# A GNN layer on one core: gathers in four parts a group with a bound lead, and 47 instead of 21 tiles fetched by row

## The chip, the core and the metric

The kernel runs on one core of one Trainium2 chip. The core has five engines with an instruction stream each: TensorE (PE in the profile; PEld is its weight load), VectorE (DVE), ScalarE (ACT), GpSimd (POOL) and SyncE (SP). They meet through semaphores. Any of SP, ACT and POOL can issue DMA transfers; the data is moved by 16 DMA engines. The metric is the device time of one execution, in microseconds (us); less is better.

## The reference

One pre-norm layer of a graph network over N = 12500 nodes of D = 256 features and E = 200000 edges, all in fp32. `dst` is sorted.

```python
h = jnp.maximum(_layernorm(x, axis=-1), 0.0)
agg = jax.ops.segment_sum(h[src], dst, num_segments=N)
z = (1.0 + eps_gin) * h + agg
t = jnp.dot(z, W1) + b1                          # 256 -> 512
t = jax.nn.relu(_batchnorm(t, g1, bt1))
conv_out = jnp.dot(t, W2) + b2                   # 512 -> 256
out = x + jax.nn.relu(_batchnorm(conv_out + h, g2, bt2))
```

The part that matters here is `h[src]` with its sum: for each of 200000 edges a row of 1 KB is fetched from a node's place and added to the edge's target.

## The kernel before

**Tiles and groups.** The edges are cut into 1563 tiles of 128 (NTILE) and the tiles into 131 groups (NG) of 12 (GT). As `dst` is sorted, a tile's edges go to few neighbouring nodes. A tile of gathered rows is 128 x 256: an edge on each partition.

**Three stretches.** The first 30 groups (LEAD) gather from `x` and normalize what they gathered, while another part of the program computes h for all nodes and writes it to a table, `h_one`. Groups 30 to 130 gather finished rows from `h_one`; this is the middle stage, from 518.4 to 2282.0 us in the profiled execution. Behind it come the batch norm, the second product and the output.

**One step of the loop (lines 826 to 879).** Step i issues the gathers of group i+4 (AHEAD = 4) on POOL (`gather`, L573), builds the one-hot matrices of group i+2 on DVE (`edges`, L635), and sums group i on PE (`sums`, L655). `sums` does one matmul for each tile, `ps += oh^T x rows`, with the one-hot matrix as weights: 12 weight loads and 12 matmuls (L672) add up in one PSUM tile `ps`. Then DVE copies `ps` to `zs` (`hold`, L726), PE places `zs` in the columns of its nodes (`put`, L733, L739) and DVE adds that to `zc` (`add`, L754), which holds h itself, loaded on SP (`z_load`, L629) and scaled on ACT (`z_scale`, L633). When a chunk of `zc` is complete PE multiplies it with W1 (`slice_of`, L764), DVE takes its moments (L775) and ACT stores it (`keep_t`, L782). `put` and `slice_of` stand among the matmuls of `sums`.

**Gathers.** A tile is one indirect DMA on POOL (L589): it reads 128 row numbers of `srcT` and writes 128 rows. A group's twelve go to one buffer of `rows_pool`, which has four (RING = 4), so POOL may be up to four groups ahead of PE. POOL does little else in the middle stage. The gathers' arrival is kept by hand: all but the last of a group count on a semaphore `inside` that nobody waits for, the last one on a semaphore of its buffer, `landing[place_of(i)]` (L516 to L521), and TensorE waits for that once ahead of a group's first matmul (`wait_for`, called at L660). `behind` tells the scheduler that this wait covers the group's tiles.

**Tiles by row.** Some tiles are fetched another way, one row at a time, by SP or ACT (`fetch`, L553). `SINGLES` (L32) says which: SP has a tile in group 33 and each ninth group from there (11 tiles), ACT in group 37 and each ninth (10): 21 tiles that POOL doesn't gather, always the group's first ones, summed last. A tile is made in four pieces of 32 rows (PIECE). A piece loads 32 byte offsets into the engine's registers (L560, a TENSOR_LOAD) and issues 32 DMAs of 1 KB (L565), each of which counts on `arrived[k]`; TensorE waits for the whole tile ahead of its matmul (L671). The pieces are due from step i-7 on (SOONER = 7), spread over the steps of one spacing (L551), behind the loads of that step. The places are the twelve tiles of two buffers that are free by then, `gta` (8) and `gtb` (4), in turn. In the profile the rows of L565 and the matmuls `ps<-gta,oh` and `ps<-gtb,oh` are these tiles.

**What sets the order.** Each engine runs its instructions in the order of the program. On SP the `zc` loads and the rows share one stream, on ACT the scaling of `zc`, the stores of `ts` and the rows.

Of the kernel before, what the change touches and what calls it, by code (L numbers as in the profile page):

```python
# [17 lines left out]
P = 128  # L18
# [4 lines left out]
AHEAD = 4  # L23
LEAD = 30
EARLY = 2
FRONT = 2
RING = 4
# [1 line left out]
XIN = 1  # L29
PIECE = 32  # L30
SOONER = 7
SINGLES = (("sync", 33, 9), ("scalar", 37, 9))  # L32


COPIES = 2
# [6 lines left out]
def kernel(  # L42
# [16 lines left out]
    nc = tc.nc  # L59
# [10 lines left out]
    for g in range(NCH):  # L70
        rows = min(CH, N - g * CH)
# [7 lines left out]
    full_tiles = E // P  # L79
    left = E - full_tiles * P  # L80
    NG = -(-NTILE // GT)
# [8 lines left out]
    h_one = dram.tile([N, D], F32, name="h_one")  # L90
# [25 lines left out]
    srcT = consts.tile([P, NBLK * P], I32, name="srcT")  # L116
# [49 lines left out]
    with ExitStack() as es:  # L166
# [5 lines left out]
        whole = E // PART  # L172
# [67 lines left out]
        for i in range(EARLY):  # L240
            for t in reversed(range(GT)):
                k = i * GT + t
                nc.gpsimd.indirect_dma_start(
                    out=slot(early[i], t), out_offset=None, in_=x,
                    in_offset=bass.IndirectOffsetOnAxis(ap=srcF if k == GT - 1 else srcE[:, k : k + 1], axis=0),
# [103 lines left out]
    def fast():  # L349

        parts = []
        for n0, w in chunks:
            n = w * R
# [20 lines left out]
        with ExitStack() as fs:  # L374
# [10 lines left out]
            h_one = dram.tile([N, D], F32, name="h_one")  # L385
# [4 lines left out]
            with ExitStack() as es:  # L390
# [122 lines left out]

                groups = [(t0, min(GT, NTILE - t0)) for t0 in range(0, NTILE, GT)]
                gathered = {i: early[i] for i in range(EARLY)}
                landing = [tc.alloc_semaphore(f"whole{k}") for k in range(AHEAD + 1 + RING)]  # L516
                inside = tc.alloc_semaphore("inside")
                uses, arrival = [0] * len(landing), {}

                def place_of(i):  # L520
                    return i % (AHEAD + 1) if i < LEAD else AHEAD + 1 + i % RING  # L521

                singles_at = [
                    (tile_, c) for tile_ in lands[0] for c in range(tile_.shape[1])
# [1 line left out]
                alone, due = {}, {}  # L526
                for name, i0, every in SINGLES:
                    for k in range(NG):
# [24 lines left out]
                def fetch(name, step):  # L553

                    eng = getattr(nc, name)
                    for i, j, q in due.pop((name, step), ()):
                        k, _ = placing[i, j]
                        place, c = singles_at[k]
                        k_line = i - opening
                        _, ats = nc.values_load_multi_w_load_instructions(  # L560
                            starts[j][k_line : k_line + 1, q : q + PIECE], engines=[eng.engine],
                            min_val=0, max_val=(N - 1) * ROW, skip_runtime_bounds_check_because="src names nodes",
                        )
                        for r, at in enumerate(ats):
                            single = eng.dma_start(  # L565
                                place[q + r : q + r + 1, c, :].bitcast(U8),
                                h_bytes[bass.ds(at, ROW)].rearrange("(o b) -> o b", o=1),
                            )
                            tc.no_tile_sem_insts.add(single.ins.name)
                            tc.add_to_no_dep_group(f"single{i}_{j}", single.ins)  # L570
                            single.then_inc(arrived[k], 16)

                def gather(i):  # L573
                    t0, n = groups[i]
                    a = len(alone.get(i, ()))
                    k = i % (AHEAD + 1)
                    if i >= LEAD:
                        pair = rows_pool.tile([P, 2 * GT, D], F32, name="gt")
                        ga = [(a, GT, pair[:, a:GT, :])]
                        for j in range(a):  # L580
                            place, c = singles_at[placing[i, j][0]]
                            ga.append((j, j + 1, place[:, c : c + 1, :]))
                    elif k < EARLY:
                        ga = early[k]
                    else:
                        ga = ((0, GT, singles[k - EARLY]),)
                    for t in reversed(range(t0 + a, t0 + n)):
                        rows = left if t == full_tiles else P
                        fetch = nc.gpsimd.indirect_dma_start(  # L589
                            out=slot(ga, t - t0)[:rows], out_offset=None, in_=x if i < LEAD else h_one,  # L590
                            in_offset=bass.IndirectOffsetOnAxis(ap=srcT[:rows, t : t + 1], axis=0),
                        )
                        if i < NG - 2:
                            tc.no_tile_sem_insts.add(fetch.ins.name)
                            tc.add_to_no_dep_group(f"rows{i}", fetch.ins)
                            fetch.then_inc(inside if t > t0 + a else landing[place_of(i)], 16)
                    if i < NG - 2:
                        uses[place_of(i)] += 1
                        arrival[i] = landing[place_of(i)], 16 * uses[place_of(i)]
                    gathered[i] = ga  # L600

                def wait_for(i, eng):

                    if i in arrival:
                        eng.wait_ge(*arrival.pop(i))
                        return True

                def behind(i, reader):

                    tc.declare_no_dep(reader.ins, group=f"rows{i}", reason="its engine waits for the group's semaphore")  # L610
                    tc.declare_fence(reader.ins, group=f"rows{i}")

                def span(i):
                    return STEP * i - MARGIN, STEP * i - MARGIN + WIDE
# [11 lines left out]
                def z_load(c):  # L626
                    n = chunks[c][1] * R
                    zc[c] = zcp.tile([P, DC, CH], F32, name="zc")
                    nc.sync.dma_start(zc[c][:, :, :n], h_cols[c, :, :, :n])  # L629
# [19 lines left out]
                def sum_place(i):  # L649
                    if not halves:  # L650
                        pair = ps_s.tile([P, 2, D], F32, name="ps")
                        halves.extend((pair[:, 1, :], pair[:, 0, :]))
                    return halves.pop()

                def sums(i, among=()):  # L655

                    t0, n = groups[i]
                    ga, oh = gathered.pop(i), ohs.pop(i)
                    waited = wait_for(i, nc.tensor)
                    ps = sum_place(i)  # L660
                    a = sum((i, j) in placing for j in range(n))
                    order = list(reversed(range(a + 1, n))) + list(reversed(range(a))) + [a]
                    at = {(k + 1) * n // (len(among) + 1): work for k, work in enumerate(among)}
                    for k, j in enumerate(order):
                        if k in at:
                            at[k]()
                        rows = left if t0 + j == full_tiles else P
                        lhsT, rhs = oh[:rows, j, :], slot(ga, j)[:rows]
                        if (i, j) in placing:
                            place, use = placing[i, j]  # L670
                            nc.tensor.wait_ge(arrived[place], 16 * P * use)  # L671
                        part = nc.tensor.matmul(ps, lhsT=lhsT, rhs=rhs, start=(j == order[0]), stop=(j == order[-1]))  # L672
                        if waited:
                            behind(i, part)
                            waited = False
                        if (i, j) in placing:
                            tc.declare_no_dep(part.ins, group=f"single{i}_{j}", reason="TensorE waits for their own semaphore")
                            tc.declare_fence(part.ins, group=f"single{i}_{j}")
                    summed[i] = ps
# [119 lines left out]
                def first(c):  # L799

                    return min(i for i in range(NG) if c in reach(i))
# [6 lines left out]
                for i in range(EARLY, min(AHEAD, NG)):  # L808
                    gather(i)
# [10 lines left out]
                for c in range(NCH):  # L820
                    k = min(max(first(c) - 2, c + 2), NG - CLOSE - 1)
# [4 lines left out]
                for i in range(NG - CLOSE):  # L826
# [49 lines left out]
                    for c in loads.get(i, ()):  # L876
                        z_load(c)
                    for name, _, _ in SINGLES:
                        fetch(name, i)
# [96 lines left out]
            with tc.tile_pool(name="ps_y", bufs=2, space=PSUM, reuse_waits="tile") as ps_y:  # L976
# [117 lines left out]
                for p in range(1, PAIRS - 1):  # L1094
                    a, b = 2 * p, 2 * p + 1
# [47 lines left out]
                a, b = 2 * p, 2 * p + 1  # L1143
# [308 lines left out]
    with tc.If(off == 0):  # L1452
        fast()
# [32 lines left out]
```

## Time and profile before

| | |
|---|---|
| runs | 2508.0, 2510.9 and 2526.5 us; median 2510.9 |
| profiled execution | 2513.2 us; its span in the profile 2511.4 us |
| mean granted clock of TensorE | 0.751 |

| stage (us) | length | POOL busy | PE busy | granted clock | DMA engines' busy share |
|---|---|---|---|---|---|
| 0 to 518.4: groups 0 to 29, h | 518.4 | 343 | 281 | 0.76 | 0.59 |
| 518.4 to 2282.0: groups 30 to 130 | 1763.6 | 1119 | 995 | 0.72 | 0.38 |
| 2282.0 to 2511.4: the rest | 229.4 | 74 | 211 | 0.98 | 0.77 |

How to read the views below. In a view by group or by timeline a row names the engine, the line, the operation, the output and inputs with the program's names, and how many; busy time and the mean of one stand beside it. `[4.52 <-remote]` behind a row is the idle time of that engine just before it and what ended it: "remote" is a semaphore from another engine that the trace can't name further, "issue" means that the engine waited for nothing that the profile shows, a name is the instruction or DMA that was waited for. A row whose engine ends in q (SPq, ACTq, POOLq) counts what the engine's queue did outside its busy time, DMA issues and waits; its numbers are the shortest, median and longest duration of one in ns, then the first and the last time. In the view of waits a row gives the waiting engine, its output and line, the releaser, the total idle time in us, how often, and the longest.

### The profile page before, as it was taken

The page shows a single profiled execution, that of the slowest core. Times are in us where ns is not written, and L with a number is a line of the kernel's source. Part 1 is how long each engine was busy: PE and PEld are TensorE (multiplying, and loading weights), DVE is VectorE, ACT ScalarE, POOL GpSimd, SP SyncE. Part 2 cuts the span into 40 slices and gives each one's busy share as a digit, 9 for nine tenths or more (in the row PEclk, how much of TensorE's full clock was granted, in tenths as well). Part 3 has the DMA queues.
Part 4 walks back from the last instruction along what each step waited for, and adds up shares of the span by engine and source line. Part 5 has one row for each costly group of instructions (what it writes and reads, how often), then busy time and mean ns, then how long its engine had stood idle before and what let it go on. Part 6 is the DMA issues. An engine that isn't in the chain of part 4 may idle for free.

```text
span 2511.4 us, 20472 instructions
## 1 busy us (share of the span) xinstructions
PE 1486.5 (59%) x4856; PEld 1016.6 (40%) x4856; DVE 860.0 (34%) x1344; ACT 419.0 (17%) x776; POOL 1536.4 (61%) x1588
## 2 busy tenths in 40 slices
PE   2456565656655655475654546555364565658997
PEld 1334343434443434343433425333252343435445
DVE  5445465532222212222221222222221222223897
ACT  4465465430000000000000000000000000001554
POOL 7666666656566666666665666656656566662550
PEclk9667787768777777676767767777676767779999
DMA  5565566533333333333333433333333333343988
GB/s 173 162 202 183 171 208 203 163 100 111 106 110 115 105 112 109 106 109 113 113 102 101 117 96 111 113 101 109 98 107 106 106 106 104 111 146 101 315 308 337
DMA packets 150561, 349.87 MB, mean 139 GB/s; under 512 B 33061, under 2 KB 63612, under 8 KB 150430
## 3 DMA queue, kind: packets, MB, share of 16 engines
q0 software_dynamic: 74000, 202.15, 28.6%
q1 hardware_dynamic: 58922, 118.77, 13.8%
q10 hardware_dynamic: 17508, 27.55, 3.0%
q8 instruction: 41, 0.67, 0.1%
q14 instruction: 90, 0.74, 0.1%
HBM read 284.33 MB, written 64.00 MB: 139 GB/s over the span
## 4 chain that ended last, share of the span: by engine, by line
issue 30%; PE 29%; ACTq 18%; another core or an unknown queue 8%; DVE 5%; ACT 4%; SPq 3%; DMA 1%; POOL 1%; DVEq 0%
ACTq L565 16%; PE ps L672 16%; PE ph L764 3%; PE pz L739 3%; SPq L565 3%; ACT gt L460 2%; PE one L1025 2%; ACTq L560 2%; PE pr L1025 1%; PE pq L1025 1%; PE ph L499 1%; DVE oh L640 1%; DVE stg L433 1%; ACTq L782 1%
## 5 line engine op out<-in xcount | busy, mean ns | idle before, releaser
L589 POOL DMA_INDIRECT gt<-h_one,srcT x1182 | 1119.3, 947 | 644.5 <-issue 348.6
L672 PE MATMUL ps<-gt,oh 128*128 128x256 f32 x2766 | 832.1, 437 | 475.6 <-issue 467.9
L672 PEld LDWEIGHTS ps<-gt,oh 128*128 128x128 f32 x2766 | 607.1, 221 | 697.9 <-issue 607.7
L726 DVE COPY zs<-ps 128x256 f32<-128x256 f32 x99 | 41.4, 418 | 814.8 <-remote 586.6
L640 DVE TENSOR_TENSOR oh<-col,dstT 128x1536 f32<-128x1536 f32 x129 | 225.6, 1750 | 238.4 <-remote 143.4
L633 ACT ACTIVATE zc<-zc,gin 128x1024 f32<-128x1024 f32 (+1 forms) x25 | 28.2, 1128 | 1537.4 <-issue 1259.4
L739 PE MATMUL pz<-at,zs 128*128 128x256 f32 x516 | 180.8, 457 | 166.1 <-issue 151.9
L589 POOL DMA_INDIRECT gt<-in_x_dram,srcT x216 | 204.6, 947 | 99.4 <-issue 45.5
L764 PE MATMUL ph<-zc,w1s 128*128 128x512 f32 (+1 forms) x392 | 209.7, 660 | 45.0 <-DVE gt L511 29.0
L739 PEld LDWEIGHTS pz<-at,zs 128*128 128x128 f32 x516 | 118.0, 230 | 215.5 <-issue 189.4
L775 DVE BATCH_NORM_STATS2 st<-ph 128x6 f32<-128x512 f32 x96 | 66.6, 693 | 266.1 <-remote 188.2
L672 PE MATMUL ps<-gta,oh 128*128 128x256 f32 x224 | 64.0, 420 | 139.5 <-DMA gta<-h_one 122.0
L754 DVE TENSOR_TENSOR zc<-pz,zc 128x512 f32<-128x512 f32 (+7 forms) x185 | 91.2, 517 | 119.6 <-remote 81.9
L764 PEld LDWEIGHTS ph<-zc,w1s 128*128 128x128 f32 x392 | 84.6, 218 | 115.2 <-issue 73.9
L460 ACT ACTIVATE gt<-gt,nbg,rsg 128x256 f32<-128x256 f32 x216 | 108.6, 592 | 10.6 <-issue 10.5
L672 PEld LDWEIGHTS ps<-gta,oh 128*128 128x128 f32 x224 | 46.5, 212 | 151.4 <-DMA gta<-h_one 125.8
L589 POOL DMA_INDIRECT gta<-in_x_dram,srcT x80 | 75.7, 947 | 37.1 <-issue 14.9
L499 PE MATMUL ph<-ident,gt 128*128 128x128 f32 x196 | 38.5, 317 | 93.3 <-issue 61.4
L672 PE MATMUL ps<-gtb,oh 128*128 128x256 f32 x106 | 40.5, 517 | 73.9 <-DMA gtb<-h_one 39.1
L499 PEld LDWEIGHTS ph<-ident,gt 128*128 128x128 f32 x196 | 26.5, 159 | 108.8 <-issue 69.1
L433 DVE BATCH_NORM_STATS2 stg<-gt 128x6 f32<-128x512 f32 x108 | 68.3, 688 | 3.2 <-DMA gt<-in_x_dram,srcT 2.6
L731 DVE TENSOR_SCALAR at<-col,shift 128x256 f32<-128x256 f32 x129 | 61.0, 474 | 1.1 <-issue 1.1
(188 smaller groups left out, 1152.2 us busy)
## 6 DMA issues: line engine op xcount, KB each, us to landing
t_tab<-ts ACTq DMA_DIRECT2D x96, 256.0 KB
gt<-h_one,srcT POOLq DMA_INDIRECT x1182
gta<-h_one SPq DMA_DIRECT2D x1024, 1.0 KB
gta<-h_one ACTq DMA_DIRECT2D x1024, 1.0 KB
gt<-in_x_dram SPq DMA_DIRECT2D x24, 512.0 KB
h_one<-gt SPq DMA_DIRECT2D x24, 512.0 KB
h_cols<-gt SPq DMA_DIRECT2D x24, 512.0 KB
zc<-h_cols SPq DMA_DIRECT2D x24, 512.0 KB
```

The source lines that it names most:

```text
L433: reader = nc.vector.bn_stats(st[:, c : c + 2, :].rearrange("p c s -> p (c s)"), two.rearrange("p c d -> p d c"),)
L460: nc.scalar.activation(slot(to, c), slot(v, c), AF.Relu, bias=nb[:, c : c + 1], scale=rs[:, c : c + 1])
L499: nc.tensor.transpose(ph[:, c * P : (c + 1) * P], ht[:, c, d * P : (d + 1) * P], ident)
L565: single = eng.dma_start(place[q + r : q + r + 1, c, :].bitcast(U8), h_bytes[bass.ds(at, ROW)].rearrange("(o b) -> o b", o=1),)
L589: fetch = nc.gpsimd.indirect_dma_start(out=slot(ga, t - t0)[:rows], out_offset=None, in_=x if i < LEAD else h_one, in_offset=bass.Indirect ...
L640: nc.vector.tensor_tensor(oh, col[:, :P].unsqueeze(1).to_broadcast([P, n, P]), dstT[:, t0 : t0 + n].unsqueeze(2).to_broadcast([P, n, P]), ...
L672: part = nc.tensor.matmul(ps, lhsT=lhsT, rhs=rhs, start=(j == order[0]), stop=(j == order[-1]))
L739: nc.tensor.matmul(pz[:, d, :n], lhsT=zs[:, d * P : (d + 1) * P], rhs=at[:, :n], start=True, stop=True)
L754: nc.vector.tensor_add(side, pz[:, :, a - lo : b - lo], side)
L764: nc.tensor.matmul(ph[:, :n], lhsT=w1s[:, d, f * P : (f + 1) * P], rhs=zc[c][:, d, :n], start=(d == 0), stop=(d == DC - 1),)
L775: nc.vector.bn_stats(st1[:, f, c, :], ph[:, :n])
L1025: nc.tensor.matmul(ps, lhsT=w[:, k, :], rhs=t[:, k, :], start=(k == 0), stop=(k == DC - 1))
```

## The change

Three things, all in the middle stage.

1. *Four parts.* A group of the middle stage is gathered in four parts (PARTS = 4) of up to three tiles. Each part has a landing semaphore of its own, and TensorE waits for a part ahead of that part's first matmul, no longer once a group.
2. *A bound lead.* TensorE counts on a new semaphore, `summed_up`, with each part that it has closed. From group 38 on (SETTLED) POOL waits ahead of each part until TensorE has closed the part five back (CLOSELY = 5). Before, only the four buffers of `rows_pool` bounded its lead.
3. *More tiles by row.* SP has a tile in group 33 and each fourth group from there (24 tiles), ACT in group 35 and each fourth (23): 47 tiles, not 21. A tile's four pieces are then due one a step, steps i-7 to i-4.

Unchanged are the number of buffers, the order of the tiles in a group, the first 30 groups and the two last ones.

```diff
+PARTS = 4
+CLOSELY = 5
+SETTLED = 38
-SINGLES = (("sync", 33, 9), ("scalar", 37, 9))
+SINGLES = (("sync", 33, 4), ("scalar", 35, 4))
...
-                landing = [tc.alloc_semaphore(f"whole{k}") for k in range(AHEAD + 1 + RING)]
+                landing = [tc.alloc_semaphore(f"whole{k}") for k in range(AHEAD + 1 + RING * PARTS)]
+                summed_up = tc.alloc_semaphore("summed_up")
...
-                def place_of(i):
-                    return i % (AHEAD + 1) if i < LEAD else AHEAD + 1 + i % RING
+                def place_of(i, part=0):
+                    return i % (AHEAD + 1) if i < LEAD else AHEAD + 1 + i % RING * PARTS + part
+
+                def parts_of(i, a, n):
+
+                    rows = list(reversed(range(a, n)))
+                    if not LEAD <= i < NG - 2:
+                        return [rows]
+                    size = -(-len(rows) // PARTS)
+                    return [rows[k * size : (k + 1) * size] for k in range(PARTS)]
...
-                    for t in reversed(range(t0 + a, t0 + n)):
...
+                    for part, members in enumerate(parts_of(i, a, n)):
+                        if SETTLED <= i < NG - 2:
+                            nc.gpsimd.wait_ge(summed_up, PARTS * (i - LEAD) + part - CLOSELY + 1)
+                        for j in members:
+                            t = t0 + j
...
+                                fetch.then_inc(landing[place_of(i, part)] if j == members[-1] else inside, 16)
...
-                    waited = wait_for(i, nc.tensor)
...
+                    opens, closes = {}, set()
+                    if i >= LEAD or (i, 0) in arrival:
+                        for part, members in enumerate(parts_of(i, a, n)):
+                            opens[members[0]] = part
+                            closes.add(members[-1])
...
+                        waited = j in opens and wait_for(i, nc.tensor, opens[j])
...
                         part = nc.tensor.matmul(ps, lhsT=lhsT, rhs=rhs, start=(j == order[0]), stop=(j == order[-1]))
                         if waited:
-                            behind(i, part)
-                            waited = False
+                            behind(i, part, opens[j])
+                        if i >= LEAD and j in closes:
+                            nc.tensor.sem_inc(summed_up, 1)
```

`wait_for` and `behind` take a part beside the group; nothing else of them changes.

More of the change, by code (lines that the diff above doesn't have):

```diff
@@ L586, in gather @@
                         ga = ((0, GT, singles[k - EARLY]),)
-                    for t in reversed(range(t0 + a, t0 + n)):
[L588 to L592, printed above, removed]
-                        if i < NG - 2:
-                            tc.no_tile_sem_insts.add(fetch.ins.name)
-                            tc.add_to_no_dep_group(f"rows{i}", fetch.ins)
-                            fetch.then_inc(inside if t > t0 + a else landing[place_of(i)], 16)
@@ L597, in gather @@
-                    if i < NG - 2:
-                        uses[place_of(i)] += 1
-                        arrival[i] = landing[place_of(i)], 16 * uses[place_of(i)]
+                    for part, members in enumerate(parts_of(i, a, n)):
[3 more added lines that the diff above has]
+                            t = t0 + j
+                            rows = left if t == full_tiles else P
+                            fetch = nc.gpsimd.indirect_dma_start(
+                                out=slot(ga, j)[:rows], out_offset=None, in_=x if i < LEAD else h_one,
+                                in_offset=bass.IndirectOffsetOnAxis(ap=srcT[:rows, t : t + 1], axis=0),
+                            )
+                            if i < NG - 2:
+                                tc.no_tile_sem_insts.add(fetch.ins.name)
+                                tc.add_to_no_dep_group(f"rows{i}_{part}", fetch.ins)
+                                fetch.then_inc(landing[place_of(i, part)] if j == members[-1] else inside, 16)
+                        if i < NG - 2:
+                            uses[place_of(i, part)] += 1
+                            arrival[i, part] = landing[place_of(i, part)], 16 * uses[place_of(i, part)]
@@ L600, in gather, with wait_for @@
                     gathered[i] = ga
-                def wait_for(i, eng):
-                    if i in arrival:
-                        eng.wait_ge(*arrival.pop(i))
-                        return True
-                def behind(i, reader):
-                    tc.declare_no_dep(reader.ins, group=f"rows{i}", reason="its engine waits for the group's semaphore")
-                    tc.declare_fence(reader.ins, group=f"rows{i}")
+                def wait_for(i, eng, part=0):
+                    if (i, part) in arrival:
+                        eng.wait_ge(*arrival.pop((i, part)))
+                        return True
@@ L613, in span, with behind @@
+                def behind(i, reader, part=0):
+                    tc.declare_no_dep(reader.ins, group=f"rows{i}_{part}", reason="its engine waits for their semaphore")
+                    tc.declare_fence(reader.ins, group=f"rows{i}_{part}")
                 def span(i):
```

## The prediction

> **What bounds the kernel now.** I read the times first, then the page's span and its 40 slices, then the busy time by stage.
>
> ```profile
> span 2511.4 us, 20472 instructions
> ...
> POOL 7666666656566666666665666656656566662550
> PEclk9667787768777777676767767777676767779999
> ...
> core 0: us, PE busy (x) PEld busy (x) DVE busy (x) ACT busy (x) POOL busy (x), PEclk, DMA share, GB/s
> 518.40:2282.00 1763.60, 994.73 (x3132) 691.13 (x3132) 411.70 (x612) 44.01 (x66) 1119.32 (x1182) 0.72 0.38 108
> 2282.00:2511.40 229.40, 210.63 (x702) 117.61 (x700) 184.25 (x244) 109.34 (x146) 74.09 (x34) 0.98 0.77 278
> ```
>
> The edit lies in the middle stage, 518.4 to 2282.0: 1763.6 us with all 1182 gathers from `h_one`. No engine is full in it: POOL is busy for 1119 us, PE for 995, the DMA engines for 38%. So I looked at what starts each gather: the costliest group, then the timeline of POOL, where I kept the first gather after each pause.
>
> ```profile
> L589 POOL DMA_INDIRECT gt<-h_one,srcT x1182 | 1119.3, 947 | 644.5 <-issue 348.6
> ...
> 1453.46 0.95 POOL L589 DMA_INDIRECT gt<-h_one,srcT  x1 [4.52 <-remote]
> ...
> 1487.97 0.94 POOL L589 DMA_INDIRECT gt<-h_one,srcT  x1 [4.78 <-remote]
> ...
> 1768.64 0.95 POOL L589 DMA_INDIRECT gt<-h_one,srcT  x1 [4.62 <-remote]
> 1786.16 0.95 POOL L589 DMA_INDIRECT gt<-h_one,srcT  x1 [2.81 <-remote]
> ...
> 2193.26 0.96 POOL L589 DMA_INDIRECT gt<-h_one,srcT  x1 [4.43 <-remote]
> 2244.34 0.95 POOL L589 DMA_INDIRECT gt<-h_one,srcT  x1 [6.28 <-remote]
> ```
>
> A gather takes 0.95 us and about 0.30 of issue, 1.25 together. From 1453.46 to 1487.97 that is 24 gathers and a pause of 4.78, from 1768.64 to 1786.16 it is 12 and 2.81, from 2193.26 to 2244.34 it is 36 and 6.28. The pause grows with the run: 34.51 / 24 = 1.438 us a gather, 17.52 / 12 = 1.46, and 51.08 / 36 = 1.419 in the last one, behind the last single row. So a gather costs 1.44 us, not 1.25, and something that it leaves behind is worked off in the pause. 1182 x 1.438 = 1700 us: POOL is the bound for all but 64 us of the stage. What the backlog does to the others stands in the timeline of one such run:
>
> ```profile
> 1461.93 1.89 PE L672 MATMUL ps<-gt,oh 128*128 128x256 f32 x8
> ...
> 1476.93 0.58 PE L672 MATMUL ps<-gt,oh 128*128 128x256 f32 x1 [2.22 <-issue]
> 1479.73 0.58 PE L672 MATMUL ps<-gt,oh 128*128 128x256 f32 x1 [2.22 <-issue]
> ...
> 1487.43 0.58 PE L672 MATMUL ps<-gt,oh 128*128 128x256 f32 x1 [1.51 <-issue]
> 1487.73 0.42 DVE L726 COPY zs<-ps 128x256 f32<-128x256 f32 x1 [19.85 <-remote]
> ```
>
> Early in the run eight matmuls take 1.89 us. Later one takes 2.8 us from start to start and waits for nothing visible ("issue"). Just as POOL's pause ends, TensorE, VectorE and POOL all go on within 0.6 us: signals too are held up until then (VectorE waited 19.85 us). The row fetches on SyncE and ScalarE go the same way. In the view of line 565 the counts are: the whole run; the first 5 us around the restart at 1768.64; the 12.2 us behind it; the last 29 us of the long run; and 7 us in which POOL stood still.
>
> ```profile
> L565 SPq DMA_DIRECT2D gta<-h_one x1024: 3/228/1412, 515.4 to 1989.9; - x171
> L565 SPq DMA_DIRECT2D gtb<-h_one x384: 3/228/1397, 1087.5 to 2167.6; - x192
> ...
> L565 SPq DMA_DIRECT2D gta<-h_one x11: 3/228/755, 1767.4 to 1771.7; - x11
> ...
> L565 SPq DMA_DIRECT2D gta<-h_one x8: 3/690/710, 1773.1 to 1784.4; - x8
> ...
> L565 SPq DMA_DIRECT2D gta<-h_one x14: 3/693/709, 1457.9 to 1485.3; - x14
> L565 ACTq DMA_DIRECT2D gtb<-h_one x12: 3/691/700, 1457.9 to 1483.9; - x12
> ...
> L565 SPq DMA_DIRECT2D gtb<-h_one x20: 12/228/686, 1343.1 to 1349.7; - x20
> ```
>
> SyncE issues about 10 rows in the 5 us around a restart, then 8 / 12.2 = 0.66 a us, in a long run 14 / 28.8 = 0.49, and 20 / 7 = 2.86 where POOL is idle. Over the stage it made 1408 rows in 1652 us, 0.85 a us, and that is late already:
>
> ```profile
> PE ps L672 <- DMA gta<-h_one: 122.0, 8, 33.7
> ...
> PE ps L672 <- DMA gtb<-h_one: 39.1, 2, 27.8
> ...
> 569.95 0.94 POOL L589 DMA_INDIRECT gt<-h_one,srcT  x1 [21.78 <-PE ps L672]
> ...
> 1990.92 0.94 POOL L589 DMA_INDIRECT gt<-h_one,srcT  x1 [14.07 <-PE ps L672]
> ```
>
> TensorE waited ten times, 161 us, for a tile fetched by row. Being up to four groups ahead, POOL lost only what went past its lead: the 64 us.
>
> **The change part by part.**
> *26 gathers leave POOL* (47 tiles, not 21): 26 x 1.438 = -37 us, on the path.
> *26 x 128 = 3328 rows come.* What a row takes from POOL's drain: the long run above held 23 rows near its start (estimated as 10 of SyncE and 13 of ScalarE) and the 26 shown, and took 34.51 us where 24 x 1.419 = 34.06 would do: 0.45 / 49 = 0.009 us a row, +30 us. Bounds: 0, if the difference is chance, and 0.028 (the 12-gather cycle: 17.52 - 12 x 1.419 = 0.49 over the 19 rows of SyncE alone, 0.026, rounded up), +93. I take 0.009, from the longer cycle. So even with no wait a row tile saves little: 1.438 - 128 x 0.009 = 0.3 us.
> *Waits on POOL and TensorE, and TensorE's increments.* Rows of such instructions, and the loads that fetch the row numbers:
>
> ```profile
> L589 POOLq EVENT_SEMAPHORE  x308: 17/17/10012, 25.8 to 2267.7; - x154
> ...
> L672 PEldq EVENT_SEMAPHORE  x1: 51/51/51, 24.1 to 24.1; - x1
> ...
> L560 SPq TENSOR_LOAD <-starts x44: 5/1564/3174, 510.2 to 2136.6; - x44
> ```
>
> POOL's 364 new waits (91 groups by 4) at 17 ns are 6 us, under the 0.30 us of issue before each gather: nothing, 6 without that cover. TensorE gets 3 more waits and 4 increments a group, 99 x 7 x 51 ns = 35 us, on an engine idle for over 700 us of the stage: nothing while POOL bounds, 35 if TensorE did.
> *POOL held.* From group 38 on it may issue a part only when TensorE has summed the part five back. Behind the wait stand POOL's next gathers; TensorE waits for them, and everything else for TensorE. POOL's lead falls from 4 groups to 5 parts, 1.25 groups. A late row tile used to be hidden by the lead; now POOL idles too, soon after TensorE stops.
> *Rows against time, the term that decides.* SyncE's 24 tiles come one in four groups. POOL's share of four groups is 46 x 1.419 + 256 x 0.009 = 67.6 us, so SyncE has to make 128 rows at 1.9 a us, over twice its present 0.85. Its supply hangs on how often POOL stops: 10 rows at each restart, 0.66 a us otherwise. How often is not shown before, so it is bounded. At most all five parts but the one just landing are free at a restart: 4 parts (12 gathers, the cycle at 1768.64), 4 restarts in four groups: 4 x 10 + (67.6 - 20) x 0.66 = 71 rows. At the other end POOL stops at every part (16 restarts, 4.2 us apart): 2.86 a us throughout, no shortage. Between, 2 parts: 8 x 10 + 27.6 x 0.66 = 98 rows. A row tile stops TensorE every two groups, and behind such a stop four parts wait for TensorE and POOL is let on by ones and twos, later by four. I take 2, 2 and 4 parts for the eight of two groups, six restarts in four: 6 x 10 + 37.6 x 0.66 = 85 rows. The tile's four loads of 1.56 us cost 4 more: 47 short of 128, made at 2.86 a us while POOL is idle: 16.6 us in four groups, over 23 spacings +382 us. With 4 parts throughout it is (57 + 4) / 2.86 x 23 = +487, with 2 throughout (30 + 4) / 2.86 x 23 = +273.
> *Queued behind the rows.* On SyncE the 25 loads of `zc`, on ScalarE the scaling of `zc` and 72 of the 96 stores of `ts`. They are due two groups early and go in the same pauses; no further price.
> The 64 us of old idle are part of the new 382, so they come off once.
> *Sum*, against the profiled execution's own 2513.2 us (0.1% above the runs' median, 2510.9): 2513.2 - 37 + 30 - 64 + 382 = 2824, I say 2820. Two parts: 2715; four: 2929. Before 518.4 and behind 2282.0 nothing changes.
>
> A rule on the clock, against a row:
>
> ```profile
> 1989.59 4.34 PE L672 MATMUL ps<-gt,oh 128*128 128x256 f32 x10
> ...
> 1994.63 4.70 PE L672 MATMUL ps<-gt,oh 128*128 128x256 f32 x21
> ```
>
> Behind its wait to 1988.6 TensorE's matmuls came at 0.43 us, five us later at 0.22. The Trainium skill, "TensorE: Matmul & The Clock Gate", section "Part 1: The HAM clock gate", says that an idle window of some 3.4 us halves the clock until a busy one restores it; these rows agree. By it 37 more waits would add, as an estimate, 37 x 1.7 = 63 us if all of it were on the path (2880). I leave it out of the sum, since after a wait POOL is let on by TensorE's first closed part.
>
> **The rivals.**
> *Faster: POOL stops so often that the slow pace never sets in.* If it is let on part by part, SyncE's tile takes 128 / 2.86 + 6.3 = 51 us of the 67.6, no row is late, and the time is 2513.2 - 37 + 30 - 64 = 2442. For it: 11 rows in 5 us around a restart, and a part is only 4.3 us. Against it: TensorE sums four tiles in 1.9 us, so it is soon close behind POOL, and then nothing holds POOL for four parts. It decides from 1.8 rows a us on (9 short: 3.1 us x 23 = 71, what was gained). Between, at 1.7 to 1.85, the time is within 1%.
> The Trainium skill, "DMA: Bandwidth & Descriptors", section "Issuing engines are not separate DMA queues", has all three queues run on the same 16 DMA engines and calls the saved issue time "usually small relative to the DMA itself"; by that alone the edit would be worth POOL's 37 us (2476). The trace has issue at 0.35 to 2 us a row, and the measurement decides.
> *The hold comes to nothing*: TensorE's increments get through at once, it is always within five parts, and POOL runs in long bursts as now. Then two restarts in four groups, 2 x 10 + 57.6 x 0.49 = 48 rows, (80 + 4) / 2.86 x 23 = +676, 3117 us. Against it: VectorE's 19.85 us wait shows such signals held up.
>
> **How the numbers follow.** Row shortage with two to four parts a stop: 0.57, 2820, own range 2690 to 2950. The faster rival: 0.28; in between, within 1%: 0.08; the hold without effect: 0.07. Some 1% is what a measurement of this kernel can tell from no change. Slower is 0.57 + 0.07 = 0.64. The range reaches from the faster rival to the upper end of the forecast, 2440 to 2950.
>
> **What would show it.** Right: the share of POOL's pauses ended by TensorE grows far past 64 us, TensorE's waits for `gta` and `gtb` stand at more than 161 us, and a group takes over 20 us. Wrong: SyncE's rows at 228 ns nearly throughout, pauses of POOL every 4 to 5 us and a stage under 1750 us; or bursts of 24 gathers as before. The cost of a gather would be wrong if POOL's starts, pauses counted, came closer than 1.42 us.

## The result and the profile after

| | before | after |
|---|---|---|
| runs (us) | 2508.0 to 2526.5, median 2517.2 (4) | 3182.2 to 3190.5, median 3184.9 (4) |
| ratio | 1 | 1.2655, 95% interval 1.2596 to 1.2714 |
| profiled execution, its span | 2513.2, 2511.4 | 3182.2, 3180.5 |

The change costs 668 us. The prediction had the sign, but its 2820 us and its range up to 2950 are too low.

First the busy time by stage in the changed kernel; the stage borders are POOL's first and last gather from `h_one`. The columns are the length, then busy time and count for each engine, the granted clock, the DMA engines' share and GB/s.

```profile
0.00:517.20 517.20, 276.41 (x1016) 205.12 (x1017) 263.35 (x489) 265.72 (x564) 343.17 (x372) 0.77 0.59 183
517.20:2951.00 2433.80, 1003.60 (x3162) 699.40 (x3160) 414.99 (x616) 44.59 (x67) 1095.82 (x1156) 0.66 0.27 79
2951.00:3180.50 229.50, 208.28 (x680) 116.20 (x680) 180.59 (x239) 108.98 (x146) 75.23 (x34) 0.95 0.77 277
```

The first and the last stretch are as before. The middle stage is 2434 us long, 670 more, and POOL is busy in it for 24 us less. So all of the loss is waiting. TensorE's granted clock is lower there, 0.66 where it was 0.72, but its busy time is 1004 us against 995, so slower matmuls are not the loss. Who waits, from the view of waits (waiting engine, its line, the releaser: us, times, longest) and the page's group of the gathers:

```profile
POOL gt L605 <- PEq L697: 939.8, 67, 37.7
...
PE ps L693 <- DMA gta<-h_one: 536.7, 29, 39.1
...
PE ps L693 <- DMA gtb<-h_one: 283.9, 14, 39.9
```

```profile
L605 POOL DMA_INDIRECT gt<-h_one,srcT x1156 | 1095.8, 948 | 1335.8 <-PEq L697 939.8
```

TensorE waits 821 us for tiles fetched by row, where it was 161, and POOL 940 us for TensorE's increment (L697), the hold. By the order in which the tiles are used, 23 of the 43 waits and 716 of the 821 us are for SyncE's tiles. In the kernel before nine of the ten waits and 149 of the 161 us were for ScalarE's. The order of cause is read from one period of four groups. In the timeline of POOL, the gathers that didn't follow at once:

```profile
1699.18 0.94 POOL L605 DMA_INDIRECT gt<-h_one,srcT  x1 [36.26 <-PEq L697]
1734.30 0.95 POOL L605 DMA_INDIRECT gt<-h_one,srcT  x1 [6.62 <-PEq L697]
...
1800.56 0.95 POOL L605 DMA_INDIRECT gt<-h_one,srcT  x1 [37.73 <-PEq L697]
```

POOL stops twice in these four groups. From 1699.18 and from 1734.30 it issues 23 gathers each without a stop. The rows that SyncE issued in this period, in four windows (1699.1 to 1727.7, the first run; to 1734.2, the pause; to 1762.8, the second run; to 1797.0, the stop):

```profile
L577 SPq DMA_DIRECT2D gta<-h_one x22: 9/228/709, 1699.1 to 1726.0; - x22
L577 SPq DMA_DIRECT2D gta<-h_one x10: 13/228/708, 1728.8 to 1733.6; - x10
L577 SPq DMA_DIRECT2D gta<-h_one x19: 3/263/702, 1736.2 to 1760.5; - x19
L577 SPq DMA_DIRECT2D gta<-h_one x77: 3/228/707, 1763.3 to 1796.9; - x77
```

Of the tile's 128 rows 41 were made in 57 us in which POOL ran, and 77 in the 34 us in which POOL stood still and TensorE came to wait for this very tile. What TensorE did meanwhile (a tile is two matmul records in the trace):

```profile
1742.04 3.62 PE L693 MATMUL ps<-gt,oh 128*128 128x256 f32 x16
...
1764.70 0.59 PE L693 MATMUL ps<-gt,oh 128*128 128x256 f32 x1 [1.53 <-issue]
1799.73 1.22 PE L693 MATMUL ps<-gta,oh 128*128 128x256 f32 x2 [34.45 <-DMA gta<-h_one]
```

It waits 34.45 us for the tile; its increment then lets POOL go on at 1800.56, and the next period begins. The last of the 128 rows was issued at 1796.9, and SyncE's next tile starts at once. From 800 to 2800 us SyncE's stream has no gap over 1.4 us. The page also follows the work back from the last instruction and gives each engine's share of the span in that chain, here for the kernel before and for the changed one:

```profile
issue 30%; PE 29%; ACTq 18%; another core or an unknown queue 8%; DVE 5%; ACT 4%; SPq 3%; DMA 1%; POOL 1%; DVEq 0%
```

```profile
SPq 47%; issue 33%; PE 11%; another core or an unknown queue 3%; DVE 3%; ACT 2%; DMA 0%; ACTq 0%; DVEq 0%
```

SyncE's queue had 3% of it and has 47%. It sets the pace of the whole stage: one tile, four groups, some 98 us here and 99.2 in the mean over 19 periods.

### The profile page after: what moved, and what is told of

Same layout as the page of the kernel before. It is cut to its first block, busy times and chain, and to the rows that moved or that the text cites. A ratio compares the mean times of both kernels' runs of the same rounds, so it can differ in the third digit from the quotient of the medians.

```text
span 3180.5 us, 27695 instructions
## 1 busy us (share of the span) xinstructions
PE 1488.3 (47%) x4856; PEld 1020.7 (32%) x4856; DVE 858.9 (27%) x1344; ACT 419.3 (13%) x776; POOL 1514.2 (48%) x1562
## 4 chain that ended last, share of the span: by engine, by line
SPq 47%; issue 33%; PE 11%; another core or an unknown queue 3%; DVE 3%; ACT 2%; DMA 0%; ACTq 0%; DVEq 0%
SPq L577 40%; SPq L572 7%; PE ps L693 4%; PE one L1047 2%; PE pr L1047 1%; PE pq L1047 1%; PE ph L786 1%; PE ph L502 1%; PE pz L761 1%; ACT gt L463 1%; DVE stg L436 1%; ACT gta L463 1%; DVE oh L656 0%; PE one L1084 0%
## 5 line engine op out<-in xcount | busy, mean ns | idle before, releaser
L605 POOL DMA_INDIRECT gt<-h_one,srcT x1156 | 1095.8, 948 | 1335.8 <-PEq L697 939.8
L693 PE MATMUL ps<-gt,oh 128*128 128x256 f32 x2714 | 797.3, 437 | 337.8 <-issue 300.3
L693 PE MATMUL ps<-gta,oh 128*128 128x256 f32 x256 | 90.2, 478 | 568.8 <-DMA gta<-h_one 536.7
L786 PE MATMUL ph<-zc,w1s 128*128 128x512 f32 (+1 forms) x392 | 235.1, 689 | 178.2 <-issue 176.4
L693 PEld LDWEIGHTS ps<-gta,oh 128*128 128x128 f32 x256 | 55.7, 232 | 609.7 <-DMA gta<-h_one 567.2
L761 PE MATMUL pz<-at,zs 128*128 128x256 f32 x516 | 152.9, 422 | 161.3 <-DVE zc L776 101.3
L693 PE MATMUL ps<-gtb,oh 128*128 128x256 f32 x126 | 51.2, 549 | 307.4 <-DMA gtb<-h_one 283.9
L761 PEld LDWEIGHTS pz<-at,zs 128*128 128x128 f32 x516 | 110.6, 217 | 190.9 <-issue 137.4
L693 PEld LDWEIGHTS ps<-gtb,oh 128*128 128x128 f32 x126 | 31.5, 272 | 329.8 <-DMA gtb<-h_one 257.4
```

Source lines behind the costliest of these rows:

```text
L605: fetch = nc.gpsimd.indirect_dma_start(out=slot(ga, j)[:rows], out_offset=None, in_=x if i < LEAD else h_one, in_offset=bass.IndirectOffse ...
L761: nc.tensor.matmul(pz[:, d, :n], lhsT=zs[:, d * P : (d + 1) * P], rhs=at[:, :n], start=True, stop=True)
L786: nc.tensor.matmul(ph[:, :n], lhsT=w1s[:, d, f * P : (f + 1) * P], rhs=zc[c][:, d, :n], start=(d == 0), stop=(d == DC - 1),)
```

## The experiments

Where nothing else is said, times stand beside runs of the kernel before of 2513 to 2532 us. Theory A is: SyncE's rows bound the stage, since they are slow while POOL runs.

**e1: the 47 tiles alone.** The kernel before with
```diff
-SINGLES = (("sync", 33, 9), ("scalar", 37, 9))
+SINGLES = (("sync", 33, 4), ("scalar", 35, 4))
```


> The kernel before, with the 47 row tiles alone: gathers a group at a time, POOL bounded only by its four buffers. Theory A (the rows bound the stage, and they are made only while POOL stands still; the hold changes little): behind a late tile POOL runs some 46 gathers on end, 65 us in which SyncE makes about 10 + 0.5 x 57 = 38 of its 128 rows; the other 90 take 31 us and the loads 5, so four groups take about 100 us and the whole 3150 to 3300 us. Theory B (the hold is what costs: POOL may no longer run ahead): without it most of the 667 us is gone, 2500 to 2750 us.

Measured: 3046 us, ratio 1.2124 (1.2083 to 1.2165). Four fifths of the loss come from the tiles alone; theory B falls. The size is missed as well: A's range began at 3150 us. A had POOL run some 46 gathers on end behind a late tile; in the trace it stops three times in four groups, after 11 gathers, then 23, then 12.

```profile
1579.98 0.94 POOL L589 DMA_INDIRECT gt<-h_one,srcT  x1 [30.84 <-PE ps L672]
1596.09 0.95 POOL L589 DMA_INDIRECT gt<-h_one,srcT  x1 [2.65 <-remote]
1629.19 0.95 POOL L589 DMA_INDIRECT gt<-h_one,srcT  x1 [4.66 <-remote]
1672.87 0.94 POOL L589 DMA_INDIRECT gt<-h_one,srcT  x1 [28.96 <-PE ps L672]
```

**e2: the parts and the hold alone.** The changed kernel with the old `SINGLES`.

> The changed kernel with the 21 row tiles of before: the four parts, their waits, the increments and the hold at five parts alone. Theory A (rows): POOL's lead of 1.25 groups hides less of TensorE's waits for row tiles; of the 161 us that TensorE waited before, 64 reached POOL, now up to all of it: 2510 to 2610 us. Theory B (the hold costs by itself): over 2900 us.

Measured: 2562 us, 1.0206 (1.0173 to 1.0239), some 50 us, inside A's bounds. 533 and 49 make 582 of the 668 us; the other 86 arise only together.

**e3: two parts instead of five.** `CLOSELY = 2` in the changed kernel.

> The changed kernel with CLOSELY = 2 instead of 5: POOL may be two parts ahead of TensorE's sums. Theory A (what counts is how often POOL stops, since SyncE's rows are made around its stops): with two parts POOL can't run 23 gathers on end any more; six to sixteen stops in four groups instead of two give 2450 to 2900 us, faster than the changed kernel although the hold is tighter. Theory B (the hold costs): slower than the changed kernel, over 3250 us. Theory C (SyncE makes rows at one pace whatever POOL does): no change, 3150 to 3250 us.

Measured: 3116 us, 1.2400 (1.2339 to 1.2462). The direction is A's, faster than the changed kernel though the hold is tighter, but the size is missed by over 200 us. From 800 to 2800 us POOL stood still for over 2 us 64 times, 3.05 times in 46 gathers, where the changed kernel has 49, 2.4 in 46; six to sixteen were expected. Two parts still let it run 26 and 15 gathers on end, then 5 up to the late tile:

```profile
1665.94 0.94 POOL L605 DMA_INDIRECT gt<-h_one,srcT  x1 [28.99 <-PEq L697]
1702.93 0.94 POOL L605 DMA_INDIRECT gt<-h_one,srcT  x1 [4.70 <-PEq L697]
1724.66 0.94 POOL L605 DMA_INDIRECT gt<-h_one,srcT  x1 [3.27 <-PEq L697]
1763.28 0.94 POOL L605 DMA_INDIRECT gt<-h_one,srcT  x1 [32.68 <-PEq L697]
```

**e5: SyncE's tiles without ScalarE's.** In the changed kernel
```diff
-SINGLES = (("sync", 33, 4), ("scalar", 35, 4))
+SINGLES = (("sync", 33, 4),)
```


> The changed kernel without ScalarE's 23 tiles: SyncE's 24 stay, one in four groups, POOL gathers the other 23 again. Theory A (each engine issues for itself, and SyncE's issue alone is short): in the changed kernel's trace SyncE made 0.757 rows a us while POOL ran and 2.05 in its pauses; 47 gathers run 58.75 us, 44 rows; the other 84 take 41 us; 99.7 us in four groups against 98.3: the same time, 3100 to 3260 us. Theory D (the 1 KB transfers of both engines together are too many for the DMA engines): half the rows, half the loss or less, 2500 to 2850 us.

Measured: 3139 us, 1.2463 (1.2364 to 1.2561). Half of the rows are gone, and 623 us of the loss stay. It isn't the number of transfers but SyncE's own issue that is short; D falls.

**e6: the parts without the hold**, 47 tiles. `SETTLED = 200` in the changed kernel.

> The changed kernel with SETTLED = 200, so that POOL is never held: four parts, their waits and increments, and 47 tiles. The changed kernel took 3185 us, the 47 tiles alone 3046. Theory A1 (the hold gives the difference: TensorE and POOL start together behind a late tile, and POOL's lead is lost): 3000 to 3090 us. Theory A2 (the parts give it: three more waits and four increments a group on TensorE): 3140 to 3230 us.

Measured: 3053 us, 1.2119 (1.2020 to 1.2217), the time of e1. The parts cost nothing that can be measured, and the hold brings the other 130 us. From the last row of one tile of SyncE to that of the next, 93.6 us go by here and 99.2 in the changed kernel (means over 19 periods of the traces); 5.6 x 23 = 129. In e1 and e6 SyncE makes 50 of a tile's 128 rows while POOL runs, in the changed kernel 43 (pauses over 2 us, from 800 to 2800 us). Fewer stops with the hold, 2.4 in 46 gathers against 3.0, would fit that, but the count alone doesn't give the time: in h1, the same changed kernel at the same time, it is 2.8, again with 43 rows, and e3 has 3.05 stops, 50 rows and 63 us more than e6. Why the hold costs SyncE these rows is not shown.

**e7: every sixth group.** The kernel before with
```diff
-SINGLES = (("sync", 33, 9), ("scalar", 37, 9))
+SINGLES = (("sync", 33, 6), ("scalar", 36, 6))
```


> The kernel before with a row tile of SyncE and of ScalarE in every sixth group (16 and 15 tiles). Theory A with the supply measured in the changed kernel (0.757 rows a us while POOL runs, 2.05 in its pauses): 70 gathers run 87.5 us, 66 rows, the other 62 take 30 us: 118 us in six groups, where POOL alone needs 102; 16 us x 15.5 spacings = 248, less the 64 us of idle time that the kernel before had already: about 2690 us (2620 to 2760). Theory E (the loss is a step: below some rate none, above it all): 2500 or 3050 us.

Measured: 2696 us, 1.0702 (1.0618 to 1.0786), where 2690 was expected. The supply measured in one kernel gives the loss at another demand; there is no step. That it came within 6 us is partly luck: in e7's own trace SyncE makes 0.84 rows a us while POOL runs and 1.66 in its pauses, not 0.757 and 2.05, and the two differences nearly cancel.

**e8: one tile only.** The kernel before with the edit below (e4, the same experiment by another edit, gave no time):
```diff
-SINGLES = (("sync", 33, 9), ("scalar", 37, 9))
+SINGLES = (("sync", 33, 9),)
...
-                    for k in range(NG):
+                    for k in range(1):
```


> The kernel before with a single row tile (SyncE's in group 33); the other 20 go back to POOL's gathers. Theory A (a row tile spares POOL only 1.438 - 128 x 0.009 = 0.3 us, and its lateness cost the 64 us of POOL's idle time): +20 x 0.3 - 64 = -58, about 2455 us. Theory C (rows cost POOL nothing and their lateness is harmless, so that each tile is worth its 1.44 us): +29 us, 2540 us.

Measured: 2471 us, 0.9813 (0.9765 to 0.9862): faster than both kernels. At this pace row tiles are worth less than they cost when late, and the fastest of all these runs at it is the one with a single tile.

**e9 and h2: POOL stopped at every part.** `CLOSELY = 1` in the changed kernel. The runs of e9 to e12, k1, k2 and m1 were made on chips on which the kernel before itself takes 2140 to 2145 us and not 2513 (more on that below), so e9 was repeated as h2.

> The changed kernel with CLOSELY = 1: POOL issues a part only when TensorE has closed the one before it, so that it stops at every part. Theory A (rows go when POOL stands still): the premise of the faster rival comes true, SyncE and ScalarE are no longer short, and TensorE's waits for gta and gtb, 821 us in the changed kernel, fall under 150 us. The time is then set by the round trip of a part, 3.75 us of issue, about 2.5 to landing and 1.5 to 3 for its sums: 8 to 9 us x 4 x 91 groups = 2900 to 3300 us in front of what stays, so 3000 to 4000 us in all. Theory F (SyncE is slow for a reason of its own, its register loads and its issue): the waits for gta and gtb stay over 500 us.

> CLOSELY = 1 as in e9, which ran at the fast pace (3014 us, no wait for gta or gtb above the 40th place) and so told nothing of the slow one. At the slow pace (kernel before at about 2513): theory A, POOL stops at every part, rows go in the stops, TensorE's waits for gta and gtb, 821 us in the changed kernel, fall under 150 us; the round trip of a part sets the time, 8 to 10 us x 364 parts, 3000 to 3900 us in all. Theory F (SyncE is slow for a reason of its own): these waits stay over 500 us. At the fast pace: 3014 us again.

Measured: 3014 us against 2140 (e9), and 3114 us against 2532 (h2), 1.2294 (1.2226 to 1.2361). The two longest groups of waits of TensorE and POOL in h2, and the one row in its view of waits that has TensorE wait for a row tile:

```profile
PE ps L693 <- DMA gt<-h_one,srcT: 1000.0, 340, 7.2
POOL gt L605 <- PEq L697: 973.2, 360, 19.8
...
PEld ps L693 <- DMA gta<-h_one: 0.2, 1, 0.2
```

With POOL stopped 16 times in 46 gathers the 821 us of waits for row tiles are gone. F falls, and SyncE's queue is down to 4% of the page's chain:

```profile
issue 29%; DMA 26%; POOL 15%; PE 11%; PEld 7%; SPq 4%; another core or an unknown queue 3%; DVE 3%; ACT 2%; PEldq 0%; POOLq 0%; ACTq 0%; DVEq 0%
```

SyncE makes a tile in 50 to 54 us where it runs on (97 in the changed kernel). The time is now that of the round trip, 973 us of POOL waiting for the part before; a part like those below takes 5.7 us, less than the 8 to 10 expected:

```profile
1643.31 0.94 POOL L605 DMA_INDIRECT gt<-h_one,srcT  x1 [2.29 <-PEq L697]
...
1648.96 0.94 POOL L605 DMA_INDIRECT gt<-h_one,srcT  x1 [2.20 <-PEq L697]
```

So rows that come in time are to be had, but at a price as high as the lateness.

**e10 and h3: the hold with one tile.** The changed kernel with the edit of e8.

> The changed kernel with a single row tile: four parts and the hold at five parts, and no late tiles. The kernel before with a single row tile took 2471 us; with 21 tiles the hold cost 2562 - 2513 = 49 us. Theory A (the hold costs only where a tile is late, since POOL then stops after five parts and not after four groups): 2455 to 2500 us. Theory B1 (the hold or the parts cost by themselves): 2510 to 2540 us.

> The changed kernel with a single row tile, as in e10 (2159 at the fast pace against 2140). At the slow pace: theory A (the hold costs only where a tile is late) 2455 to 2500 us, as the 2471 of the kernel before with one tile; theory B1 (hold or parts cost by themselves) 2510 to 2540 us. At the fast pace: 2159 us again.

Measured: 2159 us, 1.0090 (1.0074 to 1.0105) against 2140, and 2501 us, 0.9878 (0.9834 to 0.9923) against 2532. That is 1 us past A's upper bound, which had been set beside a kernel before of 2513. By ratio h3 stands 0.0065 above e8, some 16 us, and the intervals overlap: the hold costs little where no tile is late, if anything.

**e11 and h4: the parts alone, 21 tiles.** The changed kernel with the old `SINGLES` and `SETTLED = 200`.

> The changed kernel with the 21 row tiles of before and SETTLED = 200, so without the hold: the four parts with their waits and increments alone. Theory A (the 49 us of the parts and the hold with 21 tiles are the lost lead): 2500 to 2530 us, as before. Theory A2 (they are the parts' waits and increments on TensorE): 2545 to 2575 us.

> The four parts without the hold, 21 row tiles, as in e11 (2136 at the fast pace against 2140). At the slow pace: theory A (the 49 us of e2 are the lost lead) 2500 to 2530 us; theory A2 (they are the parts' waits and increments on TensorE) 2545 to 2575 us. At the fast pace: 2136 us again.

Measured: 2136 us, 0.9979 (0.9970 to 0.9988), and 2531 us, 0.9989 (0.9952 to 1.0027). The parts are free; the 49 us of e2 come from the hold.

**e12, k1 and m1: SyncE's 11 tiles without ScalarE's.** The kernel before with `SINGLES = (("sync", 33, 9),)`.

> The kernel before without ScalarE's 10 tiles: SyncE's 11 stay. In the kernel before SyncE's tiles from group 87 on were finished 2 to 4 groups early, while ScalarE's came during the sums of their own group, each one late. Theory A (a tile that is in time spares POOL 0.3 us, and ScalarE's late ones made most of the 64 us of idle time): 2471 - 10 x 0.3, so 2450 to 2480 us. Theory G (SyncE's tiles are what delays, ScalarE's harmless): 2500 us and over.

> The kernel before without ScalarE's 10 tiles, as in e12, which ran at the fast pace (2152 against 2140). At the slow pace (kernel before at about 2515): theory A (SyncE's 11 tiles come in time when spaced by nine and spare 0.3 us each, ScalarE's late ones made most of the 64 us of idle time) 2455 to 2485 us; theory G (SyncE's tiles are what delays) 2500 us and over. At the fast pace: 2152 us again.

> The kernel before without ScalarE's 10 tiles, a third time, for the slow pace (kernel before at about 2515 us): theory A (SyncE's 11 tiles come in time when spaced by nine and spare 0.3 us each, ScalarE's late ones made most of the 64 us of idle time) 2455 to 2485 us; theory G (SyncE's tiles are what delays) 2500 us and over. At the fast pace: 2152 us again.

Measured: 2152, 2153 and 2158 us, 1.0057 to 1.0061 (1.0043 to 1.0075), each time on chips where the kernel before takes 2140 to 2145 us. There ten tiles back on POOL cost 12 to 13 us, all of the 10 x 1.25 that POOL takes for them, since a gather lasts 1.25 us there. Whether the 64 us of before were ScalarE's or SyncE's late tiles these runs can't tell. The trace of before points to ScalarE's: they are nine of its ten late tiles, and ACTq has 18% of its chain where SPq has 3%. No run without them was made at that pace.

**h1 and k2: the changed kernel again.**

> The changed kernel itself once more. In the runs of e9 to e12 the kernel before took 2140 us, not 2513, and POOL issued its gathers without a pause, one in 1.25 us, and rows at 228 to 235 ns; so two paces of POOL exist. If this run has the slow pace (kernel before at about 2513): 3185 us again. If it has the fast pace (2140): theory A gives no short rows, a tile of SyncE takes 49 us of the 57.6 that POOL needs for four groups, and 26 gathers less are 26 x 1.2525 = -33 us: 2100 to 2120 us, faster than before. If rows or the hold cost by themselves, 2140 us or more.

> The changed kernel once more, for the case that the fast pace returns (kernel before at 2140 us): theory A, no row is late and 26 gathers less are 26 x 1.2525 = -33 us, 2100 to 2120 us; if rows or the hold cost by themselves, 2140 us or more. At the slow pace: 3185 us again.

Measured: h1 3186 us, 1.2581 (1.2524 to 1.2638) against 2532; k2 2122 us, 0.9916 (0.9898 to 0.9934) against 2140. On a chip of the second kind the same change is a small gain, not quite the 2100 to 2120 expected: of 33 us 18 came. TensorE still waits 69 us for 12 late tiles there, and POOL stops 10 times for 1.2 to 3.5 us, 23 us in all. By the order of use the late tiles are all ScalarE's, and each of these waits ends 19 to 21 us behind the issue of the tile's last row, where it was 2.9 us in the period shown above; why is not shown:

```profile
L577 SPq DMA_DIRECT2D gta<-h_one x2048: 221/228/1317, 435.2 to 1638.1; - x187
...
  PE ps L693: 68.6, 12
```

## Why the prediction was too low

- *The bound and the rows' pace: right.* POOL's pauses ended by TensorE are 940 us, TensorE's waits for `gta` and `gtb` 821 (161 before), a group takes 2434 / 101 = 24.1 us; all three had been named as signs. One sign of being wrong came too: "bursts of 24 gathers as before"; they have 23. e5, e7 and h2 show the cause: SyncE alone is short, by the amount that its pace gives, and no longer where POOL stops all the time. One reading behind it was wrong: the 161 us of waits before were put beside SyncE's 0.85 rows a us as its lateness, but all except 12 us of them were for ScalarE's tiles.
- *A row tile saves little: right at this pace.* e8 gave 20 tiles back to POOL and lost nothing by it, it gained 45 us; -58 came from 0.3 us a tile and the 64 us of late tiles. Where the kernel before takes 2140 us a tile saves its whole 1.25 us (e12).
- *The parts, their waits and increments at nothing: right* (e6, h4).
- *The step that failed: "At most all five parts but the one just landing are free at a restart".* From it came two to four parts a run and six restarts in four groups. But the bound of five parts moves while POOL runs. TensorE sums a part soon after it lands and its increments get through during the run. The prediction held VectorE's wait of 19.85 us against that; it did not carry over to the increments. In the changed kernel, around the run that began at 1734.30:

```profile
L697 PEldq EVENT_SEMAPHORE  x6: 51/51/51, 1734.5 to 1754.9; - x6
```

  Six increments came in the first 21 us of this run of 28.6. So POOL found each part five back already closed, until the one that held the late row tile. In this period it is stopped by a late tile each time, ScalarE's and then SyncE's, and not by its own lead: two stops in four groups, 2.4 in the mean of this trace and 2.8 in that of h1, instead of six. e3 shows how far this goes: even two parts back, TensorE keeps up.
- *What that did to the sum.* With two stops the prediction's own arithmetic gives 48 rows, a shortage of 80, and 3117 us; that case stood there as the rival "the hold comes to nothing", at 0.07. Measured: 51 rows in two runs and a pause, 77 in the stop, 3185 us. In the stop 77 rows took 34.2 us, 2.25 a us with the tile's register loads among them, where 84 / 2.86 = 29.4 us had been set for 80 rows and the loads; the two runs and the pause took 63.7 us, where 67.6 had been set. The 68 us between 3117 and 3185 are the net of such differences and weren't taken apart further.
- *The rival's form was wrong, too.* It said that the hold does nothing. It stops POOL for 940 us, and the time is 130 us over that of e6, where it isn't there. The hold costs where tiles are late (the changed kernel against e6), and little where none is (h3 against e8). How is open: fewer rows are made while POOL runs, 43 of 128 where it was 50.
- *The faster rival.* Its premise can be had (h2), its price wasn't in it: POOL let on part by part waits 2.7 us in the mean for each part, 973 us in all. A small slip stands in that rival: by its own terms 1.7 to 1.85 rows a us gives from 2.6% slower to 0.6% faster, not within 1%. Nothing else is worked out from it.

The prediction also weighed the Trainium skill, "DMA: Bandwidth & Descriptors", section "Issuing engines are not separate DMA queues", which calls the issue time that is saved "usually small relative to the DMA itself"; by that alone it had a gain of POOL's 37 us. At the pace of the predicted runs the trace does not bear that out: SyncE's queue has 47% of the chain. In k2, where SyncE's rows have a median of 228 ns, 18 us of gain agree with it better.

## What to carry to other kernels

A window that a consumer moves on while the producer runs is no bound on the length of a run: ask whether the consumer keeps up, and what stops it. Before work is moved to an idle engine, read how fast that engine issues in the same stretch while the bound engine runs, not on average, since an engine can be idle and slow. And a demand over the supply makes the supplier the clock of the whole stage: the loss is the shortage of one period times the periods, as e7 shows beside e1.

## What the runs showed of the hardware

The same kernel runs at two paces, on different chips. The kernel before took 2513 to 2532 us in the sets of runs of e1 to e8 and h1 to h4, and 2140 to 2145 us in those of e9 to e12, k and m. The first were made on chips 10, 12 and 8, the others on chips 13 and 2; no chip was seen at both paces. The groups of the gathers in the profile of before and in that of e11, whose change costs nothing:

```profile
L589 POOL DMA_INDIRECT gt<-h_one,srcT x1182 | 1119.3, 947 | 644.5 <-issue 348.6
```

```profile
L605 POOL DMA_INDIRECT gt<-h_one,srcT x1182 | 1117.4, 945 | 360.3 <-issue 360.0
...
L577 SPq DMA_DIRECT2D gta<-h_one x1024: 221/228/492, 435.6 to 1598.9; - x171
L577 ACTq DMA_DIRECT2D gta<-h_one x1024: 234/235/557, 479.5 to 1738.6; - x171
```

In e11 the idle time before gathers is 0.30 us each and nothing else: POOL issued its gathers without one pause, a gather costs 1.25 us and not 1.44, and the rows on SyncE and ScalarE took 228 and 235 ns at the median and 557 at most. The stage is shorter by the pauses. So neither the pauses nor the slow rows belong to POOL's gathers as such, and what the prediction called a backlog is there on some chips and not on others. Its cause isn't visible in the traces and stays open. The granted clock goes with it (0.877 in e11, 0.752 in h4, the same kernel), but it can't be told from these runs whether as a cause or as a result. The sign of this change hangs on that pace: 1.2655 on the one kind of chip, 0.9916 on the other.
